# A planner beside a long scan: side banks taken by name, and side work put off where a step is full

## The chip, the core and the metric

One core of a Trainium2 chip runs the whole kernel. The time is device microseconds of one execution; a comparison is made between medians. The engines are named as in the profile: PE is TensorE (PEld its weight loads), DVE is VectorE, ACT is ScalarE, POOL is GpSimd and SP is SyncE, which here only issues transfers. SBUF is the working memory and PSUM the memory that PE writes; PSUM has eight banks of 128 x 512 float32.

## The reference, cut to what matters

The input is x, 16 batches of 512 positions by 256 channels, float32. Two layers follow each other, each with a residual sum and a layer norm. The first is a state space layer that runs in both directions over the positions; the second a layer of 16 soft experts of 64 slots.

```python
def _selective_scan(u, dt, A, B, C, D, reverse=False):
    dA = jnp.einsum('bld,dn->bldn', dt, A)
    dB_u = jnp.einsum('bld,bld,bln->bldn', dt, u, B)
    ...
    dA_cum = jnp.exp(jnp.flip(jnp.cumsum(jnp.flip(dA_shift, 1), 1), 1))
    xs = jnp.cumsum(dB_u * dA_cum, 1) / (dA_cum + 1e-12)
    y = jnp.einsum('bldn,bln->bld', xs, C)
    ...
    return y + u * D

# layer 1
xr = x @ in_proj_w.T
xf, res = jnp.split(xr, [D_INNER], axis=-1)                  # 512 and 512 channels
xf = jax.nn.silu(_causal_dw_conv(xf, conv_w, conv_b))        # 4 taps
y = _ssm(xf, res, ...)
xb = jax.nn.silu(_causal_dw_conv(xf, conv_b_w, conv_b_b))
y_b = _ssm(xb, res, ..., reverse=True)
x = _layernorm(x + (y + y_b) @ out_proj_w.T)

# layer 2
logits = jnp.einsum('bnd,esd->bnes', _layernorm(x) * g + b, se)
dispatch = jax.nn.softmax(logits, axis=1)                    # over the positions
combine = softmax of logits over all 1024 slots
slots = jnp.einsum('bnd,bnes->besd', x, dispatch)
gate = jax.nn.gelu(slots @ Wg + bg); up = slots @ Wu + bu
eout = (gate * up) @ Wd + bd
x = _layernorm(x + jnp.einsum('bns,bso->bno', combine, eout))
```

## The kernel before, in words

**The scan.** The 16 states of a channel are scanned one at a time: a tile holds 128 channels (one of four chunks c) by 512 positions. `scan_part` (called four times for each batch b: forward and backward direction r, chunk pair p) goes over the states n in twos, and for each over the two chunks of its pair. One turn of this inner loop is called a step here: 16 steps to a part, 64 to a batch, 1024 in all. A step has these instructions:

- POOL makes db = du x bs (L436), for two states at once, or for one where the other comes "by diagonal" from PE.
- ACT makes the decay (L453, Exp, written to PSUM tile h) and the factor th (L455, Tanh) of each of the two states.
- DVE scans each state over the positions (L459 forward, L461 backward) and multiplies by the factor into hg (L464).
- POOL multiplies hg by cs (L465). There are four hg buffers.
- PE adds hg into the PSUM tile acc by eight transposing matmuls (`add_up`, L380). This is kept two steps behind, and frees the hg buffer.

SP loads bs and cs (three buffers each) by broadcasting transfers from a DRAM copy of B and C (L425, L426). For a few states (four of 16 in the first three batches, two of 16 later) PE makes the product du x B of two chunks by a diagonal matrix, tile hd (`by_diagonal`, L414), a step before it is scanned in place.

**PSUM.** While the scan runs, two banks are acc, three are h, and three are "side banks" (pool `m_ps`), which all other work shares through `bank(name)`. In the tail, after the last step, all eight are side banks.

**The side work.** Everything else is written as Python generators which a planner lays between the steps. A generator yields a mark at each point at which it may be interrupted: a number k (it will next take k side banks; plus GAP, 8, if it should leave a step's gap first), HOLD (it has filled banks and will read them when it goes on) or WAIT (it will read what other engines are just making). There are three queues of generators, each a `Side`:

- `prep`: what the scan itself needs next. `prep_forward` (input transposes ptx, projections pin, taps `taps`: one ACT and three DVE instructions a chunk, L198 and L204), `turn_back` and `prep_backward` (taps pb, xb), `project_unit` (px, xd and the DRAM copy of B and C), `prep_pair` (pz, softplus dt, rr, du), `turn_pair` (pdu, duT) and `prep_gate` (pres, res).
- `front`: `finish` of the batch before (transposes pyt, output projection po, layer norm, its transposes px2) and `dispatch` (logits pl, softmax et, its transposes pd and their copy dis, slots pq and their copy sl).
- `back`: `experts` of two batches (gate pg, up pu, down peo; weights by `prefetch`, three tiles ahead) and `combine` (logits cl, their transposes ctp, combination cpo, layer norm). `experts` and two `combine` are added at every odd batch from batch 3 on and at batch 14.

After the instructions of a step, `beside_scan` first lets each Side that stands at HOLD or WAIT go on (`take_up`), then lets `prep` do a piece, then `front` and `back`, whose pieces are paced by a credit. `drain` empties a queue without steps between: `prep` at the start of each part, `front` at the end of each batch.

**The banks in the planner.** A counter gives each bank tile a number. A piece starts only if the oldest bank that anyone holds (or that a tile hd holds) is less than three numbers back, counted with what the piece needs:

```python
oldest = min([x.hold for x in sides if x.hold is not None] + diags[:1], default=count[0])
if count[0] - oldest + self.need > BANKS:
    break
```

**Order.** The instructions are not issued as written: a list scheduler places them on each engine by its own estimate. `late(ins)` (`tc.keep_in_program_order`) keeps an instruction behind what was written before it. Engines then run in their order, and wait by semaphores.

**The tail.** `finish` and `dispatch` of batch 15, the last experts, and the combinations that are left run after the scan (`side_by_side`).

Of the kernel before, what the change touches and what calls it, by code (L numbers as in the profile page):

```python
# [17 lines left out]
P = 128  # L18
# [6 lines left out]
NS = 16  # L25
# [30 lines left out]
def seq_layers(tc, ident, neghalf, a, out):  # L56
# [22 lines left out]
    with ExitStack() as ctx:  # L79
# [14 lines left out]
        ps = ctx.enter_context(tc.tile_pool(name="m_ps", bufs=3, space=PSUM))  # L94
# [7 lines left out]
        BANKS = 3  # L102
        AHEAD = 8
        tail, wide = [], []
        count = [0]

        def bank(name):
            count[0] += 1
            if tail and count[0] % 8 >= 3:
                return tail[0].tile([P, 512], F32, tag="tps", name=name)  # L110
            return ps.tile([P, 512], F32, tag="mps", name=name)
# [13 lines left out]
        first_w = [load_in(c, f"pin_0_{c}") for c in range(2)]  # L125

# [68 lines left out]
        def taps(dst, src, w, c, last):  # L195

            late(
                nc.scalar.activation(  # L198
# [3 lines left out]
            for j in range(1, KW):  # L202
                o = last if j == KW - 1 else dst
                ins = nc.vector.scalar_tensor_tensor(  # L204
# [17 lines left out]
        def prep_forward(b, lo, hi, out):  # L222

            if lo == 0:
                xt = first_x.pop() if b == 0 else load_x(b)
                out["xT"] = p1.tile([P, NM, L], F32, tag="xT", name=f"xT_{b}")
                for k in range(NM):
# [7 lines left out]
                    late(nc.scalar.copy(out["xT"][:, k, :], pt))  # L235
                out["u"] = p1.tile([P, ND, L], F32, tag="xf", name=f"xf_{b}")
            xT, xf = out["xT"], out["u"]
            for c in range(lo, hi):
# [4 lines left out]
                if b == 0:  # L243
                    late(nc.scalar.activation(xf[:, c, :], xf[:, c, :], AF.Silu))
            if hi == ND:
                yield 0
                if b > 0:
                    late(nc.scalar.activation(xf, xf, AF.Silu))
                yield WAIT
                yield from project_unit(b, 0, out)  # L250

        def turn_back(b, fwd, out):
            xb = p1.tile([P, ND, L], F32, tag="xb", name=f"xb_{b}")
            for c in range(ND):
# [3 lines left out]
                nc.scalar.copy(xb[:, c, 0 : KW - 1], pb[:, 0 : KW - 1])  # L258
            out["u"] = xb

        def prep_backward(b, out):
            xb = out["u"]
            yield 0
            late(nc.scalar.activation(xb, xb, AF.Silu))
# [3 lines left out]
        def prep_gate(b, fwd, out):  # L268
            res = p1.tile([P, ND, L], F32, tag="res", name=f"res_{b}")
            for c in range(ND):  # L270
# [3 lines left out]
                late(nc.scalar.activation(res[:, c, :], pp, AF.Tanh, scale=0.5))  # L274
                yield HOLD

                late(nc.vector.scalar_tensor_tensor(res[:, c, :], res[:, c, :], 1.0, pp, ALU.add, ALU.mult))  # L277
# [6 lines left out]
        def project_unit(b, r, out):  # L284
# [12 lines left out]
            if r == 0:  # L297
                late(nc.scalar.activation(xd, px[:XW, :], AF.Identity, bias=unit))
            else:

                late(nc.scalar.activation(xd[: XB + NS, :], px[: XB + NS, :], AF.Identity, bias=unit[: XB + NS]))
                nc.scalar.copy(xd[XC:XW, :], px[XC:XW, ::-1])
# [9 lines left out]
        def prep_pair(b, r, p, v):  # L312
# [13 lines left out]
            for c, q, pz in pzs:  # L326
                dts[c] = dt = p4.tile([P, L], F32, tag="dt", name=f"dt_{q}", bufs=4)
                if len(dts) == 1:
                    act = nc.scalar.activation(dt, pz, AF.Softplus)
                    late(act)  # L330
                else:
                    with tc.high_priority():
                        nc.scalar.activation(dt, pz, AF.Softplus)
            yield HOLD
            for c, q, pz in pzs:
# [10 lines left out]
                late(nc.vector.tensor_tensor_scan(o, ins[0], ins[1], 0.0, ALU.add, ALU.max))  # L346
# [4 lines left out]
        def turn_pair(b, r, p, v):  # L351
# [10 lines left out]
            for c, pt in pts:  # L362
                duT = p4.tile([P, L], F32, tag="duT", name=f"duT_{b}_{r}_{c}", bufs=2)
                late(nc.scalar.copy(duT, pt))  # L364
# [36 lines left out]
        def scan_part(b, r, p, v, accs, done, then):  # L401
# [6 lines left out]
            def by_diagonal(n, c):  # L408

                diags.append(count[0])  # L410
# [710 lines left out]
```

## Time and profile before

| | |
|---|---|
| median of 3 runs | 5352.24 us (5351.16 to 5356.49) |
| the profiled execution, its own time | 5353.58 us |
| its span | 5351.8 us |
| mean granted PE clock | 0.901 |
| hg products (L465): first and last start | 57.4 and 5090.3 us |
| an even batch (8), an odd batch (9), the last (15) | 308.0, 326.9, 374.7 us |
| the tail after the last hg | 259.1 us |

The profile is of one execution. A group of instructions is named by line, engine, operation, what it writes and reads; a count, the busy time in sum and the mean of one follow. A line of waits reads: the engine and the instruction that was late, the engine and the instruction that released it, the sum in us, how often, and the longest. Busy times overlap between engines, and neighbouring instructions of one engine overlap a little, so that means times counts come out some per cent over the busy time. The groups of the scan's own work:

| line, engine | what | count | mean ns |
|---|---|---|---|
| L465 POOL | hg x cs | 1024 | 2369 |
| L436 POOL | db | 1024 | 2047 |
| L464 DVE | hg (from h; from hd) | 1744; 304 | 681 |
| L459, L461 DVE | scans of h | 872, 872 | 1221 |
| L455 ACT | th (forward, backward) | 1024, 1024 | 714, 712 |
| L453 ACT | h | 872, 872 | 680 |
| L380 PE | acc, 8 matmuls a step | 8192 | 291 |
| all lines, ACT | table loads, in the program | 340 | 1283 |

### The profile page before, as it was taken

What the parts mean: (1) busy time and instruction counts of PE and PEld (TensorE: products, weight loads), DVE (VectorE), ACT (ScalarE), POOL (GpSimd) and SP (SyncE); (2) the same over time, 40 slices, a digit from 0 to 9 for tenths busy, and PEclk for the clock granted to TensorE, in tenths of its full rate; (3) what the DMA queues carried; (4) which work ended last, traced back from release to release, by engine and by line L of the source; (5) the groups of instructions that cost most, each with busy time, mean ns of one, the idle gap of its engine ahead of it and who ended that gap; (6) DMA issues with size and microseconds to landing.
All of it is one profiled execution on the core that took longest, in us unless ns stands there. A gap on an engine that the chain in (4) does not pass through costs nothing. (4 is left out here: it accounts for less than half of the span.)

```text
span 5351.8 us, 74548 instructions
## 1 busy us (share of the span) xinstructions
PE 4331.0 (81%) x24529; PEld 3407.3 (64%) x24529; DVE 4551.7 (85%) x6276; ACT 4089.7 (76%) x6518; POOL 4680.8 (87%) x2537
## 2 busy tenths in 40 slices
PE   5667776897778878798787988889787887888889
PEld 3556565766567766676666766676666766566667
DVE  7999999889898899889898898988999888887722
ACT  6778878887778878788787878888787887776633
POOL 6999999989999899998999999998999989987700
PEclk7788888998989989899899988999888998989999
DMA  5444444674446744566446754467444673456454
GB/s 144 136 130 150 125 146 135 211 231 147 146 150 223 224 131 146 184 219 198 132 144 206 229 161 157 143 211 231 149 146 149 222 227 127 140 180 217 146 162 140
DMA packets 616180, 908.86 MB, mean 170 GB/s; under 512 B 84687, under 2 KB 405839, under 8 KB 615793
## 3 DMA queue, kind: packets, MB, share of 16 engines
q1 hardware_dynamic: 533828, 859.88, 51.0%
q10 hardware_dynamic: 81964, 44.22, 3.1%
q8 instruction: 195, 3.19, 0.2%
q14 instruction: 193, 1.57, 0.1%
HBM read 840.86 MB, written 63.09 MB: 169 GB/s over the span
## 5 line engine op out<-in xcount | busy, mean ns | idle before, releaser
L465 POOL TENSOR_TENSOR hg<-hg,cs 128x1024 f32<-128x1024 f32 x1024 | 2421.6, 2369 | 143.2 <-DVE hg L464 108.6
L436 POOL TENSOR_TENSOR db<-du,bs 128x1024 f32<-128x1024 f32 (+1 forms) x1024 | 2092.1, 2047 | 225.7 <-issue 78.6
L464 DVE SCALAR_TENSOR_TENSOR hg<-th,h 128x512 f32<-128x512 f32 x1744 | 1158.5, 681 | 185.3 <-PE acc L380 112.1
L380 PE MATMUL acc<-ident,hg 128*128 128x128 f32 x8192 | 1157.9, 291 | 111.1 <-POOL hg L465 88.5
L380 PEld LDWEIGHTS acc<-ident,hg 128*128 128x128 f32 x8192 | 1029.6, 152 | 290.3 <-POOL hg L465 129.1
L461 DVE TENSOR_TENSOR_SCAN h<-h,db 128x512 f32<-128x512 f32 x872 | 1044.9, 1221 | 105.0 <-ACT h L453 95.4
L459 DVE TENSOR_TENSOR_SCAN h<-h,db 128x512 f32<-128x512 f32 x872 | 1045.7, 1221 | 47.7 <-ACT h L453 46.1
L455 ACT ACTIVATE th<-rr,Ah_f 128x512 f32<-128x512 f32 x1024 | 724.2, 714 | 206.0 <-DVE hg L464 200.5
L455 ACT ACTIVATE th<-rr,Ah_b 128x512 f32<-128x512 f32 x1024 | 721.3, 712 | 148.7 <-DVE hg L464 136.2
L453 ACT ACTIVATE h<-dt,A_f 128x512 f32<-128x512 f32 x872 | 591.5, 680 | 104.8 <-DVE hg L464 101.7
L453 ACT ACTIVATE h<-dt,A_b 128x512 f32<-128x512 f32 x872 | 592.3, 680 | 88.3 <-DVE hg L464 84.8
L414 PE MATMUL hd<-dg,duT 128*128 128x128 f32 x2432 | 371.1, 302 | 83.1 <-ACT duT L364 27.1
L414 PEld LDWEIGHTS hd<-dg,duT 128*128 128x128 f32 x2432 | 342.6, 217 | 94.4 <-ACT duT L364 28.9
L699 PE MATMUL pl<-x2T,seT 128*128 128x512 f32 x512 | 285.3, 685 | 72.0 <-DVE hg L464 32.4
L823 PE MATMUL peo<-Wd,ht 128*128 128x256 f32 x1024 | 262.5, 412 | 59.2 <-DVE rr L346 38.3
L852 PEld LDWEIGHTS pg<-st,Wg 128*128 128x128 f32 x2048 | 239.6, 192 | 99.6 <-issue 91.6
L796 PE MATMUL pu<-st,Wu 128*128 128x128 f32 x2048 | 258.2, 286 | 52.9 <-DMA Wu<-in_Wu_dram 24.2
L796 PEld LDWEIGHTS pu<-st,Wu 128*128 128x128 f32 x2048 | 248.4, 200 | 64.3 <-DVE h L461 24.6
L988 PE MATMUL cpo<-ceo,ct 128*128 128x256 f32 x1024 | 249.9, 400 | 34.0 <-DVE rr L346 33.5
L906 PE MATMUL cl<-seT,cx 128*128 128x512 f32 x512 | 245.7, 620 | 37.4 <-DVE res L277 10.3
L823 PEld LDWEIGHTS peo<-Wd,ht 128*128 128x128 f32 x1024 | 207.8, 208 | 105.5 <-DVE rr L346 40.8
L852 PE MATMUL pg<-st,Wg 128*128 128x128 f32 x2048 | 263.8, 282 | 3.0 <-DMA Wg<-in_Wg_dram 2.3
(154 smaller groups left out, 6742.1 us busy)
## 6 DMA issues: line engine op xcount, KB each, us to landing
cs<-bc SPq DMA_DIRECT2D x512, 512.0 KB, 3.7
bs<-bc SPq DMA_DIRECT2D x360, 512.0 KB, 4.8
Wg<-in_Wg_dram SPq DMA_DIRECT2D x128, 512.0 KB, 5.1
Wu<-in_Wu_dram SPq DMA_DIRECT2D x128, 512.0 KB, 5.7
Wd<-in_Wd_dram SPq DMA_DIRECT2D x128, 512.0 KB, 5.7
dg<-diag_dram SPq DMA_DIRECT2D x152, 256.0 KB, 4.1
bs<-bc SPq DMA_DIRECT2D x152, 256.0 KB, 3.6
x<-in_x_dram SPq DMA_DIRECT2D x32, 512.0 KB, 4.1
```

The costliest lines, as they stand in the source:

```text
L380: ins = nc.tensor.matmul(accs[c][:, s], hc[:, j, s], ident, is_transpose=True, start=False, stop=(last and j == 1 and lc == NL - 1),)
L414: ins = nc.tensor.matmul(h[:, s], v[c][3][:, s], dg[:, s], start=True, stop=True)
L436: nc.gpsimd.tensor_tensor(db[:, :k, :], du.unsqueeze(1).to_broadcast([P, k, L]), bs[:, :k, :], ALU.mult)
L453: nc.scalar.activation(hs[j][1], dt, AF.Exp, scale=w["A"][:, c, s])
L455: nc.scalar.activation(ths[j], rr, AF.Tanh, bias=LN_1E12 / 2, scale=w["Ah"][:, c, s])
L459: nc.vector.tensor_tensor_scan(h, dec, add, 0.0, ALU.mult, ALU.add)
L461: nc.vector.tensor_tensor_scan(h[:, ::-1], dec[:, ::-1], add[:, ::-1], 0.0, ALU.mult, ALU.add)
L464: nc.vector.scalar_tensor_tensor(hg[:, j, :], th, 1.0, h, ALU.add, ALU.mult)
L465: nc.gpsimd.tensor_tensor(hg, hg, cs, ALU.mult)
L796: nc.tensor.matmul(pu[:, fc * P : (fc + 1) * P], got["Wu", e][:, k, fc * P : (fc + 1) * P], st[:, k, :, j * SL : (j + 1) * SL], start=(k = ...
L823: nc.tensor.matmul(po[:, j * DM : (j + 1) * DM], ht[:, fc, :], got["Wd", e0 + j][:, fc, :], start=(fc == 0), stop=(fc == NF - 1),)
L852: nc.tensor.matmul(pg[:, fc * P : (fc + 1) * P], got["Wg", e][:, k, fc * P : (fc + 1) * P], st[:, k, :, j * SL : (j + 1) * SL], start=Fals ...
```

## The change

The side banks get names, 0 to 2 (0 to 7 in the tail), each a tag of its own in its pool. A list `free` says which are free; `bank` takes the one that has been free longest, and a Side gives its banks back when it has read them. A piece starts if enough are free, so one that is held long is passed over. A tile hd gives its bank back at the end of the step that scans it, or before if none is free.

The calls on ACT and DVE in the side work go through `Counted`, which issues the same instruction and adds up its size. A step is full when the side work that was taken up in it passes 1900 on ACT or 1700 on DVE (a 512-wide instruction counts 576, a scan of 512 counts 1088). In a full step `front` and `back` put off what they would take up, once, to the next step; `prep` never does. `front` and `back` also take up at most once a step now: before, a step with a tile hd let each Side go on twice.

The calls that the scan itself makes, row moments and POOL's instructions are not counted.

```diff
-        ps = ctx.enter_context(tc.tile_pool(name="m_ps", bufs=3, space=PSUM))
+        ps = ctx.enter_context(tc.tile_pool(name="m_ps", bufs=1, space=PSUM))
...
-        count = [0]
+
+        free, taken = [0, 1, 2], []
 
         def bank(name):
-            count[0] += 1
-            if tail and count[0] % 8 >= 3:
-                return tail[0].tile([P, 512], F32, tag="tps", name=name)
-            return ps.tile([P, 512], F32, tag="mps", name=name)
+            i = free.pop(0)
+            taken.append(i)
+            pool = ps if i < 3 else tail[0]
+            return pool.tile([P, 512], F32, tag=f"mps{i}", name=name, bufs=1)
...
+        class Counted:
+            def __init__(self, engine):
+                self.engine, self.spent = engine, 0.0
+
+            def __getattr__(self, name):
+                def call(out, *args, **kw):
+                    size = 1
+                    for d in (args[0] if name.startswith("reduce") else out).shape[1:]:
+                        size *= d
+                    self.spent += 64 + size * (2 if "scan" in name else 1)
+                    return getattr(self.engine, name)(out, *args, **kw)
+
+                return call
+
+        scalar, vector = Counted(nc.scalar), Counted(nc.vector)
+
+        def full():
+            return scalar.spent > 1900 or vector.spent > 1700
...
             late(
-                nc.scalar.activation(
+                scalar.activation(
...
             def by_diagonal(n, c):
 
-                diags.append(count[0])
                 made[n, c] = h = bank(f"hd_{b}_{r}_{n}_{c}")
+                diags.append(taken.pop())
...
                     nxt_n = n if c == chunks[0] else n + 2
+                    own = [diags.pop(0)] if k == 1 else []
                     if nxt_n + 1 in ds:
-                        for x in sides:
-                            x.take_up()
+                        take_up()
+                        if not free:
+                            free.append(own.pop())
                         by_diagonal(nxt_n + 1, chunks[1] if c == chunks[0] else chunks[0])
                     beside_scan()
-                    if k == 1:
-                        diags.pop(0)
+                    free.extend(own)
                     add_up(2)
...
             def go(self):
 
-                at = count[0]
                 mark = next(self.gens[0][1], None)
-                self.wait = mark == WAIT
-                if mark == HOLD:
-                    self.hold = at if self.hold is None else self.hold
+                self.held += taken
+                taken.clear()
+                self.hold, self.wait = mark == HOLD, mark == WAIT
+                if self.hold:
                     return
-                self.hold, self.gap, self.need = None, False, 0
+                free.extend(self.held)
+                self.held, self.gap, self.need = [], False, 0
...
-            def take_up(self):
-                self.took = self.hold is not None or self.wait
-                if self.took:
-                    self.go()
+            def take_up(self, may_wait=False):
+                self.took = self.hold or self.wait
+                if not self.took:
+                    return
+                if may_wait and self.put_off < 1:
+                    self.put_off += 1
+                    return
+                self.put_off = 0
+                self.go()
...
-                    oldest = min([x.hold for x in sides if x.hold is not None] + diags[:1], default=count[0])
-                    if count[0] - oldest + self.need > BANKS:
+                    if self.need > len(free):
                         break
...
+        def take_up():
+
+            prep.take_up()
+            for x in sorted((front, back), key=lambda x: -x.put_off):
+                if not x.asked:
+                    x.asked = True
+                    x.take_up(may_wait=full())
+
         def beside_scan():
-            for x in sides:
-                x.take_up()
+            take_up()
             prep.piece()
             for x in (front, back) if front.credit > back.credit else (back, front):
                 x.paced_piece(gaps=not hurry)
+            for x in (front, back):
+                x.asked = False
+            scalar.spent = vector.spent = 0.0
...
-        tail.append(ctx.enter_context(tc.tile_pool(name="t_ps", bufs=5, space=PSUM)))
+        tail.append(ctx.enter_context(tc.tile_pool(name="t_ps", bufs=1, space=PSUM)))
...
-        BANKS = 8
+        free.extend(range(3, 8))
```

`drain` and the tail's `side_by_side` call `take_up` of each Side without leave to wait, as before. All side calls on ACT and DVE are now issued from one line, that of `Counted`.

## The prediction

> **What bounds the kernel now.** I read the busy times first, then the waits of all engines by total, then the busy times stage by stage, then the order of work in one bad stretch, then the chain that ended last. Batches end where the last product hg of their 64 steps ends on GpSimd.
>
> ```profile
> PE 4331.0 (81%) x24529; PEld 3407.3 (64%) x24529; DVE 4551.7 (85%) x6276; ACT 4089.7 (76%) x6518; POOL 4680.8 (87%) x2537
> ```
> ```profile
> DVE hg L464 <- PE acc L380: 112.1, 95, 6.4
> POOL hg L465 <- DVE hg L464: 108.6, 55, 6.8
> ...
> DVE h L461 <- ACT h L453: 95.4, 93, 3.2
> ...
> POOL db L436 <- issue: 78.6, 36, 3.9
> POOL db L436 <- DVE h L459: 78.2, 48, 5.4
> ...
> DVE h L459 <- ACT h L453: 46.1, 31, 3.6
> ```
> ```profile
> 2497.40:2805.40 308.00, 242.38 (x1280) 183.36 (x1279) 282.37 (x385) 248.01 (x414) 295.25 (x157) 0.89 0.45 140
> 2805.40:3132.30 326.90, 283.53 (x1740) 230.61 (x1739) 283.91 (x397) 262.23 (x399) 295.23 (x157) 0.94 0.68 214
> 4718.00:5092.70 374.70, 315.16 (x1834) 253.44 (x1835) 282.21 (x412) 261.15 (x416) 288.05 (x151) 0.91 0.57 183
> 5092.70:5351.80 259.10, 242.51 (x1252) 183.44 (x1251) 67.18 (x191) 89.37 (x162) 14.67 (x44) 0.98 0.49 152
> ```
>
> The four stretches are batch 8, batch 9, batch 15 and the tail; the columns are length, busy PE, weight loads, DVE, ACT, POOL, granted clock, DMA share, GB/s. In the scan POOL is the busiest engine: 295.25 us of work in an even batch and 295.23 in an odd one. Yet the even one takes 308.0 us and the odd one 326.9: POOL idles 12.8 and 31.7 us, and 86.7 us in batch 15. Over the whole scan it idles 225.7 us before db and 143.2 before hg, 369 us in all. That is the most that any reordering of the scan can win. In the tail PE is busy 242.5 of 259.1 us: a second bound.
>
> The releasers above say what POOL waits for: DVE, which itself waits for PE's accumulation (112.1 us) and for ACT's decays. In batch 9 alone, DVE's wait of hg for acc sums to 12.7 us, in batch 8 to under 1, in batch 15 to 27.6. How that goes is seen here (batch 9; start, length, idle before in brackets):
>
> ```profile
> 3092.72 1.88 PE L699 MATMUL pl<-x2T,seT 128*128 128x512 f32 x4
> ...
> 3094.44 1.04 PE L380 MATMUL acc<-ident,hg 128*128 128x128 f32 x8
> ...
> 3098.44 1.12 PE L847 MATMUL pg<-ident,bg_rows 64*128 64x512 f32 x2
> ...
> 3099.49 2.05 PE L852 MATMUL pg<-st,Wg 128*128 128x128 f32 x16
> ...
> 3101.38 1.04 PE L380 MATMUL acc<-ident,hg 128*128 128x128 f32 x8
> ...
> 3102.45 1.29 DVE L464 SCALAR_TENSOR_TENSOR hg<-th,h 128x512 f32<-128x512 f32 x2 [2.37 <-PE acc L380]
> ...
> 3103.87 2.36 POOL L465 TENSOR_TENSOR hg<-hg,cs 128x1024 f32<-128x1024 f32 x1 [2.60 <-DVE hg L464]
> ```
>
> Between two accumulations PE, which works in order, does two whole tiles pg. The accumulation at 3101.38 is late, so its hg buffer (one of four) is late, so DVE idles 2.37 us and POOL 2.60. So what matters is how long the blocks of side matmuls between two accumulations are, and how much side work DVE and ACT get in a row.
>
> **The change, part by part.** The numbers come from the order in which both programs' instructions stand on each engine, and from stepping both planners through their 1024 steps; costs are this profile's group means. The instructions are the same on PE, DVE, POOL and SP; ACT alone loses 18 table loads (340 to 322).
>
> *1. Held banks passed over.* The old planner refused a piece for want of banks 530 times, the new one 350. Experts and combinations move ahead by some two steps (pg by 2.3, cpo by 1.9), preparations by half a step (pz by 0.8). At the end of the scan combination 13 is further on: of its tiles cl, ctp and cpo the tail keeps two fewer each. Prices, from the chain of the tail (cl, two tiles, 3.44; cpo 3.45 to 3.46 each) and the page's mean for two ctp (1.30): 3.44 + 1.30 + 2 x 3.46 = 11.7 us. PE sets the tail and idles only 16.6 us in it, so I take -11.7 (bounds 0 and -11.7). The same work goes into batch 15, where PE has 59.5 us free; I cost it at nothing there, and at +11.7 if that cover is gone.
>
> ```profile
> 5240.47 3.44 PE cl L906 x8
> ...
> 5316.08 3.45 PE cpo L988 x16
> ```
>
> *2. Blocks on PE.* With a tile's cost as busy time over number of tiles (pg 3.19, peo 4.10, pq 3.72, px 4.43, cl 1.92, pl 2.23 us and so on), side blocks longer than 8 us between accumulations fall from 42 to 18 in batches 3 to 14, those over 9 us from 6 to none. The time beyond 5 us (about one step) falls by 29% in each odd batch (41.4 to 29.6) and by half in an even one (20.3 to 9.8); batch 15 stays (45.7 and 46.7). DVE's wait for acc scaled so: 12.7 x 0.29 x 6 odd batches = 22, and under 1 x 0.52 x 6 even ones = 3. I take -25. Bounds: 0, if DVE is late for other reasons anyway, and -112.1, the whole row.
>
> *3. Table loads.* ACT has three fewer in each odd batch (31 to 28; batch 3 five), two more in the tail: 20 x 1283 ns = 25.7 us of ACT's work in the scan. ACT is no bound (262 of 327 us); it counts where DVE waits for it. In batch 9 those waits for h and th sum to 13.1 us. I take a third of 3.85 us in six odd batches, -8 (bounds 0 and -25.7). The Trainium skill (ScalarE: Activation LUTs, What ACT_TABLE_LOAD costs) adds about 1380 ns of drain to each load; by its 2.66 us part 3 would have 53 us of ACT's work and -17. Here no drain is seen: the load at 3098.78 starts 0.02 us after the activation before it ended, and the measurement decides.
>
> *4. Steps that get fuller.* Put-offs happen 71 times in all (54 of them in finish and dispatch), since "full" counts only side work. Preparations run earlier and are never put off. So the fourth step of every batch from the fourth on now gives DVE the gate product and two whole tap triples: 0.682 + 6 x 0.740 = 5.12 us of side work, where no step from there on had over 4.4. Side work in a batch's first four steps rises from 6.1 to 8.3 us (odd) and 6.5 to 7.3 (even): 6 x 2.2 + 6 x 0.8 = 18 us. The four hg buffers hide part: I take half, +9 (bounds 0 and +18).
>
> *5. Front is later.* Finish and dispatch run one to two steps later (pl by 1.4, pq by 1.7), so at each batch's end four rounds of them are emptied out with no scan step between, where two were: 24 more. Each adds at most pd and its copy, 0.71 + 0.58 = 1.29 us, in a chain: 31 us if all is exposed, 0 if all is hidden. After the same kind of round at 3130 us (pq, then sl) POOL shows no idle, so I take +5.
>
> *6. At no cost.* Weight, slot and bias loads and expert stores move with their pieces on SP's queue. Of 512 intervals between two cs loads, 79 held four or more other issues, now 104, but with six or more it is 19 in both; bs and cs, three buffers each, hide that; uncovered, each of 25 costs one issue of 0.3 to 0.6 us ahead of a bs. On ACT's queue the stores x1, x2T and slots, on POOL's queue the row factors, only go later with finish; POOL's scan products wait behind a factor if its moments are late (2.7 us in all before hg now). The names do not tie a tile to a place: a tile called mps0 lies in any of the three physical banks in both programs, and the DVE reader that frees a bank stands on average 2.30 steps ahead of PE's next writer, now 2.27. The gates' order, POOL's work and the scan's own instructions stay.
>
> [...]
>
> **The sum.** -11.7 - 25 - 8 + 9 + 5 = -30.7 us. The profiled span is 5351.8 us, with 1.8 around it to the 5353.58 of its own run; the median of three is 5352.24, 0.4 above the span. 5351.8 - 30.7 + 0.4 = 5321.5, say 5322 (-0.6%).
>
> **Rivals.**
>
> *Larger gain.* The earlier experts and shorter blocks free the odd batches of what sets them apart from the even ones: 6 x (31.7 - 12.8) = 113, with the tail 125: 5227. For it: PE is the engine that differs most between the two (283.5 and 242.4). Against it: in batch 9 POOL's longest waits before db come from DVE's scans, 9.9 and 5.5 us, which part 4 doesn't lighten.
>
> *Nothing.* POOL's idle only moves; parts 2 and 3 give 0, 4 and 5 cost 14, the tail gives 12: 5354. For it: only 71 put-offs, and DVE's work per batch is the same.
>
> *Slower, by the start of the batch.* The fourth step's 5.12 us on DVE comes right behind the rounds of part 5, with hg buffers already in use. Both are then paid whole, 18 + 31 = 49, parts 2 and 3 give nothing because DVE is the late one, and batch 15 pays what the tail wins: 5352 + 49 = 5401. It decides once parts 4 and 5 together cost over 45 (= 25 + 8 + 12). For it: POOL already idles before hg and db in a batch's first ten steps, and DVE's busy share (87% in batch 9) is near POOL's (90%). Against it: POOL's four-deep buffer and ACT's 20% idle time.
>
> **How the numbers follow.** Forecast 0.48, larger gain 0.13, nothing 0.13, slower 0.26. The forecast's own bounds (parts 1 to 5 at their ends) run from 5352 - 150 = 5202 to 5352 + 61 = 5413, but no part is likely at its end; 5245 to 5395 leaves out half of the larger gain and half of the slower case. About 0.2% (10.7 us) can be told from no change here. The forecast reaches that bound in nearly all of its cases: faster 0.60, same 0.14, slower 0.26.
>
> **What would show it.** Part 1: a tail some 12 us shorter after the last hg, with 10 tiles cpo. Part 2: DVE's wait of hg for acc near 87 us instead of 112.1, and odd batches under 323 us. Part 3: 322 loads and smaller waits of h for ACT. Part 4: POOL idle at each batch's fourth to sixth step, up by 1 to 2 us. Part 5: the wait of hg for acc not concentrated at a batch's start. The prediction is wrong if odd batches stay at 327 us (parts 2 and 3 void), if even batches pass 312 (parts 4 and 5 paid whole), or if batch 15, with 87 us of idle and the most changed order, moves by more than 15 us either way.

## The result, and the profile after

The changed kernel takes 5439.7 us (median of 4 runs, 5430.16 to 5444.29), the kernel before 5351.7 in the same session (4 runs): a ratio of 1.0159, 95% interval 1.0145 to 1.0174. It is slower by 88 us, or 1.6%; forecast was 5322, and the range ended at 5395. The profiled execution has a span of 5428.4 us, 76.6 more than before.

The page of the changed kernel, busy times and POOL's two main groups (sum, mean ns, then POOL's idle time ahead of them):

```profile
PE 4374.3 (81%) x24529; PEld 3431.0 (63%) x24529; DVE 4554.4 (84%) x6276; ACT 4069.2 (75%) x6500; POOL 4681.4 (86%) x2537
...
L486 POOL TENSOR_TENSOR hg<-hg,cs 128x1024 f32<-128x1024 f32 x1024 | 2418.3, 2365 | 134.6 <-DVE hg L485 90.0
L457 POOL TENSOR_TENSOR db<-du,bs 128x1024 f32<-128x1024 f32 (+1 forms) x1024 | 2087.9, 2044 | 322.7 <-issue 110.3
```

POOL works as long as before (4681.4 for 4680.8). ACT works 20 us less: the 18 table loads are gone. PE is busy 43 us longer (4374.3 for 4331.0) with the same 24529 matmuls; the second place below shows where. What grew is POOL's idle time before db, 225.7 to 322.7; before hg it fell a little, 143.2 to 134.6. Together 369 became 457: these 88 us are nearly all of what the scan lost (its last hg ends at 5183.9 instead of 5092.7, 91.2 later). The tail went the other way, 259.1 to 244.5.

By stage (batch 8, batch 9, batch 15, tail; columns as in the prediction):

```profile
2532.10:2844.50 312.40, 249.77 (x1304) 189.48 (x1304) 282.38 (x385) 248.64 (x415) 294.83 (x157) 0.89 0.44 138
2844.50:3183.60 339.10, 286.74 (x1716) 231.05 (x1717) 284.35 (x398) 258.71 (x397) 295.54 (x157) 0.92 0.65 206
4806.90:5183.90 377.00, 322.43 (x1880) 260.82 (x1879) 287.44 (x421) 260.85 (x417) 288.01 (x151) 0.93 0.58 183
5183.90:5428.40 244.50, 229.32 (x1198) 173.46 (x1196) 63.92 (x182) 88.93 (x158) 14.66 (x44) 0.97 0.52 161
```

The even batch lost 4.4 us (308.0), the odd one 12.2 (326.9), batch 15 2.3 (374.7), at the same DVE and POOL work and less ACT work. From batch 4 to 13 the even ones lost 2.0 to 5.3 us and the odd ones 7.9 to 16.6. The waits of the changed kernel that answer to those of before (sum, times, longest):

```profile
DVE h L482 <- ACT h L474: 134.9, 57, 9.4
DVE hg L485 <- PE acc L401: 119.0, 63, 5.6
POOL db L457 <- issue: 110.3, 50, 3.9
...
POOL db L457 <- DVE h L480: 102.7, 63, 7.8
POOL db L457 <- DVE h L482: 95.9, 30, 10.3
...
POOL hg L486 <- DVE hg L485: 90.0, 54, 7.7
...
DVE h L480 <- ACT h L474: 78.6, 54, 6.2
```

The row that part 2 was to shrink, DVE's hg for acc, stands at 119.0 (112.1 before). The rows that grew are DVE's scans waiting for ACT's decay h, 95.4 + 46.1 = 141.5 to 213.5, and POOL's db waiting for those scans. The longest of each, 9.4 and 10.3 us, belong together, as the next section shows.

**Two places.** POOL's gaps, laid out by step over the odd batches 5 to 13 (mean per batch), grew by 13.5 us; 12.3 of them fall on two steps out of 64. At the fourth step of the first part they went from 1.8 to 7.8 us, at the fourth step of the second part from 3.5 to 9.8. The other 62 steps gain or lose up to 3.1 us each (+18.7 and -17.5) and nearly cancel. Over all batches there are about 36 us at the first place (the even batches add 0.6 each) and 35 at the second: 71 of some 90. The row "issue" above, in which the profile names no releaser, grew by 32 us (78.6 before); its largest growth is at the eighth step of the last part, 3.1 us in an odd batch and 1.9 in an even one, and it was not explained.

*First place*, batch 9 of the changed kernel (start, length, engine; all side calls have the line L139):

```profile
2856.08 0.68 DVE L139 TENSOR_TENSOR res<-res,acc 128x512 f32<-128x512 f32 x1
...
2856.68 1.54 DVE L139 SCALAR_TENSOR_TENSOR pb<-xf,cw_b,pb 128x511 f32<-128x511 f32 x2
...
2859.74 1.23 DVE L480 TENSOR_TENSOR_SCAN hd<-dec,hd 128x512 f32<-128x512 f32 x1 [1.52 <-PE hd L435]
2860.88 0.72 DVE L139 SCALAR_TENSOR_TENSOR xb<-xf,cw_b,pb 128x509 f32<-128x509 f32 x1
2861.51 0.75 DVE L139 SCALAR_TENSOR_TENSOR pb<-xf,cw_b,pb 128x511 f32<-128x511 f32 x1
2861.68 0.16 ACT L139 COPY xb<-pb 128x3 f32<-128x3 f32 x1 [2.75 <-DVE xb L139]
...
2863.30 0.73 DVE L139 SCALAR_TENSOR_TENSOR pb<-xf,cw_b,pb 128x510 f32<-128x510 f32 x1
...
2864.54 0.74 DVE L139 SCALAR_TENSOR_TENSOR xb<-xf,cw_b,pb 128x509 f32<-128x509 f32 x1
...
2866.49 4.68 POOL L457 TENSOR_TENSOR db<-du,bs 128x1024 f32<-128x1024 f32 x2 [7.84 <-DVE h L480]
```

This is the step that part 4 foretold: the gate product res and two whole tap triples (pb, pb, xb) on DVE. POOL can't overwrite db before DVE has scanned it, and stands for 7.84 us. ACT's small copy, in order, waits 2.75 us for DVE's tap. In batch 9 of the kernel before, POOL's wait at this step is short:

```profile
2818.58 4.67 POOL L436 TENSOR_TENSOR db<-du,bs 128x1024 f32<-128x1024 f32 x2 [1.48 <-issue]
```

PE's tile hd, for which DVE waits 1.52 us, is late by a stretch in which the granted PE clock was low (changed kernel, columns as by stage):

```profile
2855.50:2858.90 3.40, 3.40 (x19) 3.40 (x17) 2.68 (x5) 3.40 (x6) 2.61 (x2) 0.50 0.98 288
```

Eight matmuls of acc with diagD take 1.91 us in this stretch, and 1.06 at the same place in e9, where the clock is 1.00. So up to 1.5 of the 6.0 us are the clock's.

*Second place*, some 90 us later:

```profile
2945.62 0.60 ACT L139 ACTIVATE x<-x,m_sh,m_rs 128x256 f32<-128x256 f32 x1
...
2946.12 0.50 ACT L139 ACTIVATE xn<-x,m_r 128x256 f32<-128x256 f32 x1
...
2946.69 1.28 ACT L139 ACT_TABLE_LOAD   x1
2947.98 0.60 ACT L139 ACTIVATE ht<-pg 128x512 f32<-128x512 f32 x1
...
2948.09 3.46 PE L889 MATMUL pg<-st,Wg 128*128 128x128 f32 x16
2948.48 0.50 ACT L139 ACTIVATE xn<-x,m_r 128x256 f32<-128x256 f32 x1
...
2951.59 0.60 ACT L139 ACTIVATE ht<-pg 128x512 f32<-128x512 f32 x1 [2.62 <-PE pg L889]
...
2952.60 1.28 ACT L474 ACT_TABLE_LOAD   x1
...
2953.90 0.69 ACT L474 ACTIVATE h<-dt,A_b 128x512 f32<-128x512 f32 x1
...
2954.69 1.23 DVE L482 TENSOR_TENSOR_SCAN h<-h,db 128x512 f32<-128x512 f32 x1 [9.40 <-ACT h L474]
...
2958.83 2.37 POOL L457 TENSOR_TENSOR db<-du,bs 128x1024 f32<-128x1024 f32 x1 [10.33 <-DVE h L482]
```

ACT has the layer norm of finish (x, xn), two table loads and two gelus ht in a row; the second gelu waits 2.62 us for PE's tile pg. The scan's decay h stands behind all this from 2945.6 to 2953.9. DVE waits 9.40 us for h, and POOL 10.33 for DVE. In the kernel before, the gelu pair stood two to three steps ahead of the layer norm (batch 9; h follows the last xn at once):

```profile
2882.50 0.60 ACT L872 ACTIVATE ht<-pg 128x512 f32<-128x512 f32 x1
...
2900.59 1.31 ACT L668 ACTIVATE xn<-x,m_r 128x256 f32<-128x256 f32 x3
2901.80 0.67 ACT L453 ACTIVATE h<-dt,A_b 128x512 f32<-128x512 f32 x1
```

The wait for pg is not in all batches. In batches 3 and 5 of the changed kernel the second gelu doesn't wait, and POOL idles 7.6 us; in 7, 9, 11 and 13 it waits 2.6 us, and POOL idles 10.3. The granted PE clock makes this difference (batch 5, batch 9):

```profile
1637.20:1644.00 6.80, 5.75 (x34) 4.11 (x35) 1.92 (x2) 6.73 (x12) 6.63 (x6) 1.00 0.53 165
2944.30:2951.10 6.80, 6.80 (x26) 5.07 (x25) 0.88 (x2) 4.60 (x9) 4.20 (x3) 0.50 0.74 192
```

The 16 matmuls of pg that the second gelu waits for take 3.46 us in batch 9, and 2.05 at full clock. Over the whole program pg's matmuls with Wg are busy 309.5 us, for 263.8 before. So some 11 of the second place's 35 us (4 x 2.7) come from PE's clock.

The meeting of gelus and layer norm isn't enough for a loss either. In the version with banks alone (e1, below) the pair stands at the same step among the layer norm, and POOL waits little:

```profile
2943.45 1.09 ACT L139 ACTIVATE ht<-pg 128x512 f32<-128x512 f32 x2
...
2951.07 2.37 POOL L457 TENSOR_TENSOR db<-du,bs 128x1024 f32<-128x1024 f32 x1 [3.23 <-DVE h L482]
```

ACT's line without an h is no shorter there (8.9 us from the end of th at 2938.1; 7.3 in batch 5 of the changed kernel, 10.0 in batch 9). But POOL had products to make until 2947.8, when the next h had already begun (2947.03); in batch 9 of the changed kernel it ran out at 2948.5, 5.4 us before h. So how far DVE and POOL are ahead counts as much as the line.

### The profile page after: what moved, and what is told of

Read it like the earlier page. It is cut to its first block, busy times and chain, and to the rows that moved or that the text cites. A ratio compares the mean times of both kernels' runs of the same rounds, so it can differ in the third digit from the quotient of the medians.

```text
span 5428.4 us, 74440 instructions
## 1 busy us (share of the span) xinstructions
PE 4374.3 (81%) x24529; PEld 3431.0 (63%) x24529; DVE 4554.4 (84%) x6276; ACT 4069.2 (75%) x6500; POOL 4681.4 (86%) x2537
## 5 line engine op out<-in xcount | busy, mean ns | idle before, releaser
L486 POOL TENSOR_TENSOR hg<-hg,cs 128x1024 f32<-128x1024 f32 x1024 | 2418.3, 2365 | 134.6 <-DVE hg L485 90.0
L457 POOL TENSOR_TENSOR db<-du,bs 128x1024 f32<-128x1024 f32 (+1 forms) x1024 | 2087.9, 2044 | 322.7 <-issue 110.3
L485 DVE SCALAR_TENSOR_TENSOR hg<-th,h 128x512 f32<-128x512 f32 x1744 | 1156.0, 679 | 191.2 <-PE acc L401 119.0
L480 DVE TENSOR_TENSOR_SCAN h<-h,db 128x512 f32<-128x512 f32 x872 | 1041.6, 1218 | 87.1 <-ACT h L474 78.6
L889 PEld LDWEIGHTS pg<-st,Wg 128*128 128x128 f32 x2048 | 284.4, 222 | 108.0 <-issue 81.0
L889 PE MATMUL pg<-st,Wg 128*128 128x128 f32 x2048 | 309.5, 314 | 2.8 <-DMA Wg<-in_Wg_dram 2.8
L943 PE MATMUL cl<-seT,cx 128*128 128x512 f32 x512 | 258.6, 643 | 44.3 <-DVE rr L139 31.9
L736 PE MATMUL pl<-x2T,seT 128*128 128x512 f32 x512 | 262.2, 637 | 33.0 <-DVE rr L139 16.3
L860 PEld LDWEIGHTS peo<-Wd,ht 128*128 128x128 f32 x1024 | 196.0, 199 | 115.9 <-DMA Wd<-in_Wd_dram 44.9
L768 PE MATMUL pq<-dis,xn 128*128 128x256 f32 x1024 | 249.5, 399 | 9.5 <-ACT dis L139 6.8
L833 PE MATMUL pu<-st,Wu 128*128 128x128 f32 x2048 | 246.5, 277 | 12.3 <-DMA Wu<-in_Wu_dram 5.2
```

The costliest lines, as they stand in the source:

```text
L457: nc.gpsimd.tensor_tensor(db[:, :k, :], du.unsqueeze(1).to_broadcast([P, k, L]), bs[:, :k, :], ALU.mult)
L480: nc.vector.tensor_tensor_scan(h, dec, add, 0.0, ALU.mult, ALU.add)
L485: nc.vector.scalar_tensor_tensor(hg[:, j, :], th, 1.0, h, ALU.add, ALU.mult)
L486: nc.gpsimd.tensor_tensor(hg, hg, cs, ALU.mult)
L860: nc.tensor.matmul(po[:, j * DM : (j + 1) * DM], ht[:, fc, :], got["Wd", e0 + j][:, fc, :], start=(fc == 0), stop=(fc == NF - 1),)
L889: nc.tensor.matmul(pg[:, fc * P : (fc + 1) * P], got["Wg", e][:, k, fc * P : (fc + 1) * P], st[:, k, :, j * SL : (j + 1) * SL], start=Fals ...
```

## The experiments

Each was compared with the kernel before on the same chip; the kernel before had medians of 5348.64 to 5355.28 us there, so gains are read from the column "over before" (median less that of before). The two last columns are POOL's idle time at the two places, mean per odd batch, from the profiled execution.

| run | median us | over before, us | ratio to before, 95% interval | first | second |
|---|---|---|---|---|---|
| before | 5351.7 | 0 | 1 | 1.8 | 3.5 |
| after | 5439.7 | 88.0 | 1.0159 [1.0145, 1.0174] | 7.8 | 9.8 |
| e1 banks by name alone | 5396.23 | 41.0 | 1.0080 [1.0065, 1.0095] | 2.3 | 3.2 |
| e2 banks, once a step | 5440.25 | 85.0 | 1.0156 [1.0141, 1.0171] | 0.2 | 3.2 |
| e3 put off, once a step, old bank rule | 5454.06 | 98.8 | 1.0188 [1.0168, 1.0208] | 1.2 | 1.2 |
| e4 after, experts later | 5403.43 | 48.2 | 1.0088 [1.0073, 1.0103] | 7.8 | 1.9 |
| e5 after without once a step | 5458.57 | 106.0 | 1.0194 [1.0179, 1.0209] | 1.2 | 8.1 |
| e6 after, edge copy on DVE | 5409.53 | 57.0 | 1.0106 [1.0091, 1.0121] | 7.9 | 7.7 |
| e7 before, tanh for gelu | 5292.59 | -60.0 | 0.9892 [0.9874, 0.9911] | 1.8 | 2.7 |
| e8 after, tanh for gelu | 5344.84 | -7.7 | 0.9986 [0.9977, 0.9995] | 7.8 | 4.0 |
| e9 after, spread taps | 5357.02 | 8.4 | 1.0013 [1.0004, 1.0023] | 4.0 | 3.0 |
| e10 after, spread taps, shift | 5361.28 | 12.6 | 1.0022 [1.0012, 1.0031] | 4.0 | 0.8 |
| e11 before, edge copy on DVE | 5339.38 | -9.3 | 0.9986 [0.9977, 0.9995] | 2.2 | 2.2 |
| e12 after, all three | 5331.05 | -17.6 | 0.9963 [0.9949, 0.9977] | 4.9 | 1.3 |
| e13 before, spread taps | 5386.66 | 33.0 | 1.0060 [1.0043, 1.0076] | 1.3 | 0.0 |
| e14 banks alone, spread taps | 5380.87 | 27.2 | 1.0045 [1.0030, 1.0060] | 0.9 | 2.8 |
| e15 after, spread taps, edge copy | 5363.97 | 10.3 | 1.0017 [1.0005, 1.0028] | 5.0 | 2.7 |
| e16 put off alone, spread taps | 5377.39 | 23.7 | 1.0038 [1.0023, 1.0053] | 0.1 | 0.4 |

**One part at a time (e1, e2, e3).**

```diff
 e1, e2:
-            return scalar.spent > 1900 or vector.spent > 1700
+            return False
 e1 too:
-                if not x.asked:
-                    x.asked = True
-                    x.take_up(may_wait=full())
+                x.take_up(may_wait=full())
 e3: counter, rotating tiles and the rule of before, with Counted, put off and asked of after
```

> The changed kernel with only the banks by name: nothing is put off, and a Side may again go on twice in a step with a tile hd. Theory Q (passing over held banks is what costs: it moves experts some two steps ahead, where their two gelus fall among finish's eight layer norm activations, and leaves fewer banks free for hd): about 5430, 5415 to 5450, with DVE waiting 8 us or more for ACT's h at the fourth step of the second part of odd batches, as in the changed kernel. Theory P (putting off, with finish later and four rounds emptied at a batch's end, is what costs): 5335 to 5360, like before.

> The changed kernel with nothing put off, but front and back still take up only once a step. Theory Q: 5415 to 5450, as e1_banks. Theory P: within 15 us of 5352 if the putting off is what costs, near 5440 if the once a step is.

> The other half: the old bank counter and rule, with putting off and once a step. Theory Q: 5345 to 5380. Theory P: 5420 to 5445, like the changed kernel.

Banks by name alone cost 41 us. With the limit of once a step they cost 85, as much as the whole change. The old bank rule with the rest costs 99, of which 19 are a longer tail (278.0 for 259.1). So neither part is innocent, and the parts don't add. Neither theory held: e1 lies between the two ranges, e3 above both, and e2's 5440 fits either. None of the three shows the two places: every partial version loses its time elsewhere. e2, for example, has 5.1 us more at the first step of an odd batch's last part.

**The second place moved (e4).** The credit of `back` starts lower in odd batches. On ACT the first three gelu pairs of an odd batch now stand at its 9th, 17th and 26th step in place of the 8th, 15th and 20th. The layer norm stays at the 19th and 20th.

```diff
-                self.left, self.credit = scan_steps, 0.0
+                self.left, self.credit = scan_steps, -1.1 if self is back and scan_steps == 128 else 0.0
```

> The changed kernel, with the experts' first piece held back by 1.1 credits (about two steps), so that in odd batches their gelus fall four steps away from finish's layer norm activations, while all else of the change stays. If the meeting of gelus and layer norm on ACT costs the odd batches what they lost at that step (POOL's idle there rose from 3.5 to 9.4 us in each of six): 5440 - 36 = 5404, and POOL's idle at that step back under 4 us. If the idle only moves to the next meeting: 5430 to 5450.

Some 40 us came back, and the idle time at the second place fell from 9.8 to 1.9 us; the first place stayed. Both were expected. But the place gives 45 us over the six odd batches, and POOL's idle time in all fell by only 25 (457 to 432) in the profiled executions: other steps of the odd batches took up part of it. ACT had 48 table loads more (370 for 322), 62 us of work in all, and the kernel was faster: where the loads stand counted more than how many there are.

**Once a step taken back (e5).**

```diff
-                if not x.asked:
-                    x.asked = True
-                    x.take_up(may_wait=full())
+                x.take_up(may_wait=full())
```

> The changed kernel, in which front and back may again take up twice in a step with a tile hd (and so may put off in the one and go on in the other); names for the banks and the putting off stay. Theory R (the limit of once a step is itself dear, whatever the putting off does): the 44 us by which the run with both banks and limit (5440.25) lies over the one with banks alone (5396.23) go, 5396. Rival S (the 44 us came from where b15 and the odd batches' gelu pairs happen to fall, so a third order has its own price): a time away from 5396 by more than 15 us, with batch 15 not back at the 352 us of the run with banks alone.

5458.57, slower than the change itself: theory R is out. With put off in place the limit is not dear; the 44 us between e1 and e2 are the price of another order. The first place is gone here (1.2 us), the second stays (8.1), and even batches are 322.0 us instead of 312.7. The double triple has only moved: in even batches two whole triples now stand in the sixth step, where POOL idles 3.7 us more than before. A small idle time at the fourth step therefore doesn't mean that the triples are apart. In e3 (1.2 us there) five of the six taps stand in that step in most batches, in batch 9 with two scans between them. e2, without the putting off, has one triple a step up to batch 13 (0.2 us).

**Who is late at the first place (e6).**

```diff
-                scalar.copy(xb[:, c, 0 : KW - 1], pb[:, 0 : KW - 1])
+                nc.vector.tensor_copy(xb[:, c, 0 : KW - 1], pb[:, 0 : KW - 1])
```

> The changed kernel with the copy of three columns xb<-pb given to DVE, behind the tap that it waited for on ACT. If ACT's wait in order for DVE's last tap is what makes the start of the odd batches late (part 0, fourth step: 6.0 us more POOL idle than before, six odd batches), up to 6 x 6 = 36 us go: 5404, and POOL's idle time at that step returns to what it was. If th is late there because DVE itself is late (gate product and two triples of taps in one step), nothing moves: 5440, within 10.

I had read ACT's 2.75 us wait as the cause. The first place didn't move, and there DVE still has everything ahead of the scan (e6, same columns):

```profile
2858.57 0.16 DVE L279 COPY xb<-pb 128x3 f32<-128x3 f32 x1
2858.64 2.34 DVE L480 TENSOR_TENSOR_SCAN h<-h,db 128x512 f32<-128x512 f32 x2
...
2859.95 4.69 POOL L457 TENSOR_TENSOR db<-du,bs 128x1024 f32<-128x1024 f32 x2 [7.82 <-DVE h L480]
```

So DVE itself is late there, as the expectation's second half says; its 5440 was a miss. The time fell by 30 us all the same (21 of them show in the profiled spans, 2 us per odd batch at the second place and the rest in many small gaps): a wrong place with the right amount. At the second place batches 7 to 13 idle 7.6 us here, not 10.3, since the stretch of low clock no longer falls on pg. By its time alone e6 would have passed for a proof.

**Gelu without its table (e7, e8).**

```diff
-                    args = (ht.rearrange("p f s -> p (f s)"), pg, AF.Gelu)
+                    args = (ht.rearrange("p f s -> p (f s)"), pg, AF.Tanh)
```

> The kernel before with tanh in the place of the experts' gelu (the values differ), which needs no table of its own: 192 table loads in the program, 340 before; an odd batch has 12 for 31, so ACT has 19 x 1.283 = 24.4 us less to do there. If ACT's bursts at the gelu pairs already set part of the odd batches' 327 us, these fall towards the even ones' 308; DVE's waits of h for ACT (141.5 us) halve: about 5300. If PE's blocks set them, the time stays within 15 us of 5352.

> The changed kernel with the same tanh: 192 table loads in the program, 322 before, 12 for 28 in an odd batch (20.5 us less of ACT). Theory A (the change's loss is that ACT gets its gelu pair with two loads and other side work in one go): the distance to the kernel before with tanh falls from 87 us to under 45, since the 6.3 us at the fourth step of the second part (6 x 6.3 = 38) and the smaller ones at the other gelu pairs go. Rival: the loss has nothing to do with the loads, and the distance stays 75 to 95.

The kernel before gains 60 us, the changed one 95; the distance shrinks from 88 to 52, not quite to the 45 that was asked for. In the kernel before, DVE's waits of h for ACT fell from 141.5 to 123.5 us and not by half. At the second place 5.8 of 9.8 us go (0.8 of 3.5 in the kernel before), at the first nothing. The 36 us by which the distance shrank are about what the second place holds; the low clock falls elsewhere on pg here, so this is not the loads alone. The table loads around the gelus thus cost something in both kernels, but more where they stand in line with other work of ACT.

**Spread taps (e9), with the shift (e10), and the control (e13).**

```diff
             for c in range(ND):
-                yield 1
+                yield GAP + 1
                 pb = bank(f"pb_{b}_{c}")
...
                 scalar.copy(xb[:, c, 0 : KW - 1], pb[:, 0 : KW - 1])
+                yield WAIT
```

> The changed kernel, in which the four tap triples of turn_back stand in steps of their own (a WAIT after each, and a gap before the next), so that a batch's fourth step has the gate product and one triple on DVE, not two. Part 4 in its own step: if DVE's 5.12 us there are what POOL's db waits for (7.8 us at that step in odd batches, 3.9 in even ones; before 1.6 and 3.2), six odd batches get back up to 6 us each and the even ones up to 1: 5440 - 36 - 6 = 5398. Rival: the taps only move and hold up db elsewhere, or PE's late hd (DVE waits 1.4 us for it there) is the cause: 5430 or more.

> Spread taps, and the experts begun four steps later as in the run with the shift. If the two places (fourth step of the first part, DVE; fourth step of the second part, ACT) are separate causes, their gains add: 36 for the shift and what the spread taps alone show, to some 5362 to 5370; that is within 15 us of the kernel before, so the two places are nearly all of the loss. Rival: the stall goes to the next late thing, and the sum is under half, 5400 or more.

> The kernel before with the four tap triples in steps of their own: the control to the changed kernel with them. If the double triple of the changed kernel is what cost it 83 us, the kernel before, which has one triple a step already, gains nothing: 5350 within 10, or loses a little as later work is pushed back. If spread taps are good in themselves, it gains 30 or more, 5320 or less, and the 83 us say nothing about the change.

One triple a step gives back some 80 of the 88 us. That is twice what was asked of the first place, and both places show why: POOL's idle time falls by 38 us at the first and 46 at the second, over all batches. First place of batch 9 in e9:

```profile
2824.95 0.72 DVE L139 SCALAR_TENSOR_TENSOR xb<-xf,cw_b,pb 128x509 f32<-128x509 f32 x1
2825.59 2.34 DVE L481 TENSOR_TENSOR_SCAN h<-h,db 128x512 f32<-128x512 f32 x2
...
2828.01 2.36 POOL L458 TENSOR_TENSOR db<-du,bs 128x1024 f32<-128x1024 f32 x1 [3.64 <-DVE h L481]
```

Both scans follow the first triple at once, and db comes after 3.64 us instead of 7.84. Second place of the same batch:

```profile
2906.17 1.09 ACT L139 ACTIVATE ht<-pg 128x512 f32<-128x512 f32 x2
...
2907.14 1.30 ACT L139 ACTIVATE xn<-x,m_r 128x256 f32<-128x256 f32 x3
...
2908.46 1.28 ACT L475 ACT_TABLE_LOAD   x1
...
2909.76 0.69 ACT L475 ACTIVATE h<-dt,A_b 128x512 f32<-128x512 f32 x1
...
2914.48 2.36 POOL L458 TENSOR_TENSOR db<-du,bs 128x1024 f32<-128x1024 f32 x1 [3.43 <-DVE h L483]
```

The gelus still stand among the layer norm, but both follow each other without a wait for pg, and the granted clock is 1.00 at the first place and while pg is made. In batch 7, where a stretch of clock 0.50 falls on the first place, POOL idles 5.2 us there, for 3.6 in the other odd batches. So e9 doesn't separate the triples from the clock. The rest of the order moved with the taps. DVE's waits for h fell from 213.5 to 161.2 us (142 before), and POOL's idle time before db to 225.3 (225.7 before); the wait for acc rose again, 119.0 to 138.3. The shift on top (e10) wins nothing, since its place is already mended: the figure expected came out (5361.28, at the lower end), but by no sum of two gains, which would have been 5321. In the kernel before (e13) the same edit loses 33 us (interval 23 to 41). So the 80 us are no gain that any order would have.

**Do the partial versions suffer from the same thing (e14, e16)?**

> Banks by name alone, with spread taps. Its fourth step holds POOL up by 2.3 us in odd batches (before 1.8), so there is no double triple to undo. If its loss of 41 us is of another kind than the start of the batch, it stays: 5385 to 5400. If the taps matter there too, 5365 or less.

> The old counter and rule for banks, with the putting off and the limit of once a step, and spread taps. Its fourth step holds POOL up by 1.2 us, no double triple; of its 99 us, 19 are a longer tail. If its loss is the later front and no matter of the batch's start, it stays: 5440 to 5455. If the taps matter there too, 5420 or less.

The same edit gives banks alone 14 us, between the two halves of its expectation, and put off alone 75 (odd batches 333.4 to 320.6), so there the taps mattered, as its second half has it. Its "no double triple" was read from POOL's idle time; DVE's order has five of the six taps in the fourth step of most batches (5.1 us of side work in an even one, 3.6 to 4.9 in an odd one), and e16 has two to four. What falls most per odd batch is idle time at the third step, 3.3 us. Which stalls make up the 75 us was not followed up; e1's 41 and e3's 99 us stay unexplained in detail.

**A version that beats both (e11, e12, e15).** The copy of e6 in the kernel before (e11), all three edits in the changed one (e12), and e12 without the shift (e15):

> The kernel before, with the three-column copy xb<-pb on DVE instead of ACT. In the changed kernel this won 30 us, though the idle time at the batch's fourth step stayed (7.9 us). If what it won is ACT's wait in order at all four triples, in both kernels alike, 10 to 30 us go here too: 5322 to 5342, and it beats both. If it is peculiar to the changed order, 5352 within 8.

> Spread taps, shift and the copy on DVE together. If all three add (36 + what the spread taps show + 30), under the kernel before: 5330 to 5345. If the copy's gain was the same stall as the spread taps', no better than the run with two of them.

> The changed kernel with spread taps and the copy on DVE, without the shift. The shift gave nothing once the taps were spread (5361 for 5357), so without it the three-part run's 5331 should come back or better: 5322 to 5332. If the shift and the copy only work together, 5345 or more.

The copy alone is worth 0.14% to the kernel before (9 us, interval 3 to 12), just under the 10 that were asked for. All three edits make the changed kernel the fastest with gelu, 5331 us, 0.37% under the kernel before (interval 0.23 to 0.51%): the scan is back where it was (5090.9 for 5092.7) and the tail keeps its gain (238.3 for 259.1). Without the shift (e15) 28 us of it go, so that expectation's 5322 to 5332 missed, although the shift gave nothing to e9. The three edits do not add.

## Why the prediction was wrong, point by point

- **Part 1, the tail (-11.7): right.** It became 14.6 us shorter, 3 more than the sum's bound, by the mechanism given: work that passed a held bank was done in the scan, and the tail has 10 tiles cpo for 12. Batch 15, costed at nothing, grew by 2.3 us.
- **Part 2, blocks on PE (-25): wrong, it gave nothing.** By the costs of the kernel before the blocks are shorter in the order, and yet the row of DVE's hg for acc went from 112.1 to 119.0. The failed step is the scaling of a wait with the length of blocks over 5 us. Two things in the runs speak against it. A tile's cost isn't fixed: at the low clock the second place's block, pres and two tiles pg, takes 11.3 us of PE, where the same tiles took 8.2 in the kernel before. And the row doesn't follow the time: in e9, some 80 us faster than the changed kernel, it is 138.3; in e8, where ACT's rows fall to 160.9, it is 142.7. Why it rises there is not shown.
- **Part 3, table loads (-8): wrong sign.** 18 loads went, and DVE's waits for h rose by 72 us; no run takes away the 18 loads alone. The step was "ACT is no bound (262 of 327 us)", with the loads costed by their number. ACT executes in order, so what counts is how much side work stands in one line ahead of h, waits for PE included. e4 shows it from the other side: 48 loads more and some 40 us less. The Trainium skill (PSUM — Partial Sum Buffer, Engine vs sequencer instructions) has the rule: the queues of ScalarE, VectorE and GpSimdE are strict FIFO. The trace agrees, with 2.62 us of waiting for pg ahead of h, through which h, that needs nothing from pg, stood.
- **Part 4, fuller fourth step (+9, bounds 0 and +18): right place, a quarter of the size.** POOL lost about 36 us there. The sum counted DVE's extra work (2.2 us for an odd batch) and halved it for the buffers of hg. But db waits for the scan, which stands behind that work and behind an hd that is late at the low clock (1.52 us); hg's buffers don't cover that, and db's wait wasn't priced. Bounds from busy time alone were too narrow.
- **Part 5, emptied rounds (+5): about right, not tested alone.** POOL's idle time in the first three steps of batches 4 to 14 sums to some 8 us, and to nothing before.
- **Not in the sum: the second place**, 35 us. The coincidence of the gelu pair with finish's layer norm stood in the order of ACT's instructions. The prediction named the side work that ACT gets in a row as what matters, but no part priced it. Some 11 of the 35 us are the low clock on pg, which no part had either. The rival by the start of the batch (5401) came nearest: its 18 + 31 us were about 36 + 8, so its sum was near by luck in its terms, and batch 15 did not pay what the tail won. Without the second place the time would still be near 5405, so the range fails by both places together.
- The signs named for "wrong" came true: odd batches above 327 us, even ones past 312. The 9.9 and 5.5 us that the prediction calls POOL's longest waits before db in batch 9 are sums of five and three waits, the longest of them 3.5; they stood in no part of the sum, and it is these waits that grew.

Shown: where the time is lost (POOL's gaps by step), that the second place's wait is for ACT's line with the gelu pair (the trace, e4 and e8), and that DVE and not ACT's copy is late at the first (e6). Argued: that the double triple alone makes the first place, since e9 changes the clock there too. Not separated: how much the stretches of low clock cost; up to 1.5 us per odd batch at the first place and 2.7 in four of six at the second can be read from the trace, some 20 of the 71 us, and no run holds the clock fixed. Not explained: the odd batches' remaining gaps, the even batches' 4 us, of which no single step holds more than 1.9, and why each partial version loses 41 to 106 us without both places.

## What to carry to other kernels

Price a reordering by what each engine gets in one line between two instructions of the critical loop, its waits for other engines included, and not by counts or busy shares: here an engine that is busy for 75% of the time held the scan for 35 us, some 11 of them by a slow tile of PE in its line. Look at the granted clock of the very stretch as well, since the mean (0.901 and 0.898) doesn't show it. Then look at the place: sum the gaps of the bound engine by loop step and compare the two kernels step by step. With a planner as finely balanced as this, the parts of a change don't add, so an edit's worth holds only in the order it was measured in; run the control in the other kernel too.

## What the runs showed of the hardware that was not expected

- Moving 64 copies of 0.16 us from ACT to DVE, the busier of the two (85% to 76%), made both kernels faster, by 9 us and by 30. The copy's own time is 10 us in all. In ACT's line it waited for DVE's tap (2.75 us in the lines above); that this wait is what the move won is not shown, since POOL's idle time at that place stayed.
- 148 table loads (340 to 192) were 190 us of ACT's work and 60 us of the kernel's time before, 130 were 167 and 95 in the changed kernel: a third of a load's 1.283 us reached the end in one order, over half in the other.
- The granted PE clock was not a level but came in stretches: 0.50, mostly for 3.4 or 6.8 us, and 1.00 between them. The same 16 matmuls took 2.05 us in the one and 3.46 in the other, and whether a stretch fell on pg changed POOL's idle time from 7.6 to 10.3 us.
